# Output blocks moved into the arm of the row count, and an eviction moved into the next chunk, in a mixture-of-experts kernel

## The chip, the cores and the metric

The kernel runs on one core of one Trainium2 chip. The metric is the device time of one execution in microseconds (us), as the median of several executions. In profiles the engines are PE (TensorE, matmuls), PEld (its weight loads, which overlap the matmuls), DVE (VectorE), ACT (ScalarE), POOL (GpSimd, which also issues the indirect DMAs here) and SP (SyncE, which issues the direct DMAs). Each engine runs its own queue of instructions, and they wait for one another by semaphores.

## The reference, cut to what matters

Eight sequences of 256 tokens, 2048 tokens of width 512, all in float32, pass a gated cross-attention and then a mixture of 16 experts of which each token takes 4:

```python
x = x + tanh(g_xattn) * sigmoid_attention(layernorm(x), ctx, ctx)
xf = layernorm(x).reshape(2048, 512)
t = xf * rsqrt(mean(xf * xf) + EPS) * norm_w
vals, idx = top_k(t @ gate_w.T + gate_b, 4)
G = zeros(2048, 16).at[rows, idx].set(softmax(vals))
h = einsum('mh,eoh->emo', t, w1) + b1          # o: 2 x 512
a = minimum(h[..., ::2], 7); b = clip(h[..., 1::2], -7, 7)
act = a * sigmoid(1.702 * a) * (b + 1)
y = einsum('emi,edi->emd', act, w2) + b2
out = x + tanh(g_ffn) * einsum('me,emd->md', G, y)
```

The kernel computes each expert only for the rows that chose it, so how many rows each expert has is known only while it runs.

## The kernel before, in words

**Stages.** The first 157 us are attention, sequence by sequence, with the routing in between: each token's four experts and gates are written into a table in DRAM, sorted by expert. Two experts' first 384 rows ("early", three blocks of 128 each) follow until 226 us, while the engines also work out the plan of the rest. The rest is done in *chunks*. A chunk is up to 512 rows (four blocks of 128, `R = 4`) of one expert. The plan gives each chunk its expert, its number of blocks and its number of rows rounded up to a multiple of 16, from 256 to 512 (17 sizes, `SIZES`). There is code for 31 chunks (`MAXC`); the first 16 always run, the others inside nested `tc.If(used > c)`. With these inputs 22 run, with 448, 400, 416, 400, 384, 368, 480, 480, 288, 448, 256, 272, 288, 336, 256, 288, 256, 272, 384, 288, 256 and 320 rows.

**Plan** (L895 to L1019, on DVE, with the last early expert's matmuls beside it on PE). For each list entry it forms the row's address (`ids`, L985) and gate (`gts`, L989), turns both by PE transposes (L991, L992, into `pid`) so that a block's 128 entries lie down a column, and writes them out as `idsG` for fetching (L994), `idsT` for delivering (L998) and `gtsT` (L1000). Rows that a block does not have get an address beyond the output, and a DMA leaves such rows out. `meta` holds, for each chunk, the size's number, the number of blocks, the expert and whether it is used.

**One chunk** (`chunk(c)`), in the order of the program, which is written out by hand (`tc.manual_schedule`), so that every engine's queue has it:

- POOL gathers the next chunk's rows by four indirect DMAs (`fetch`, L1037) into `xg`.
- DVE copies the expert's bias (L1115).
- `tc.Switch` (L1118) over the 17 sizes, on PE, DVE and ACT. Each arm holds `hidden` for four column blocks `n`: 8 groups of 4 float32 matmuls (L299; in the trace a float32 matmul is two records, so a chunk has 64) with the arm's row count as their width, each group into one of the four PSUM tiles `h0` to `h3` in turn; then the evictions on DVE and ACT (L308, L316, L317, L325) into `act`. Each engine jumps into its arm and at the end out of it (the jumps bear L1213).
- SP loads w1 of the chunk after next but one (`load_hidden`, L254, 2 MB) once `hidden` has left its slot. Three slots of weights are held (`SLOTS = 3`).
- `turn`: 16 PE transposes (L284) of the next chunk's rows, evicted by four DVE multiplications (L285) into `xT`, which the next chunk's `hidden` reads.
- `expect(c + 1)` (L1061): each engine reads the next size from `meta` and gives its sequencer a hint of the arm to come.
- `output`: for each block k, `combine` (L334, 4 matmuls of 128 rows by 512 columns, 8 records, into PSUM tile `h`k), the bias added by DVE (L342, into `yb`), the gate multiplied by ACT (L347, into `yo`), and the rows added to the output in DRAM by an indirect DMA from POOL (`deliver`, L351). Block 0 always runs; blocks 1 to 3 stand each under `tc.If(blocks > k)` (L1087), and where the block is missing its Else issues four matmuls of one column on zeros (`skip`, L1066, "blanks" below). A last block with 64 rows or fewer costs a whole block.
- SP loads w2 and its bias for the chunk after next but one (`load_output`, L261 1 MB and L266 256 KB).

So PE's order in a chunk is hidden, turn, blocks 0 to 3, and the next chunk's hidden; the four PSUM tiles `h` are shared by hidden and the blocks.

Of the kernel before, what the change touches and what calls it, by code (L numbers as in the profile page):

```python
# [31 lines left out]
def kernel(  # L32
# [35 lines left out]
    SIZES = list(range(2 * P, R * P + 1, GRAIN))  # L68
    ROWS = E * NT

    out_rows = out.rearrange("b d n -> (b d) n")

# [26 lines left out]
        "yb": (moe, [P, H], 2),  # L99
        "yo": (moe, [P, H], 3),  # L100
# [33 lines left out]
    blank = const.tile([P, P], mybir.dt.bfloat16, name="blank")  # L134
    nc.vector.memset(blank, 0.0)
# [10 lines left out]
    )  # L146
    eps = const.tile([P, 1], F32, name="eps")
# [69 lines left out]
    for tag in ("xT", "act"):  # L217
        nc.gpsimd.memset(buf(tag, 0), 0.0)
# [110 lines left out]
    def combine(slot, k, lo):  # L329

        py = buf("h", k)
        act = buf("act", 0)
        for i in range(IC):
            nc.tensor.matmul(  # L334
                py,
                act[:, i, lo : lo + P],
                w2r[:, slot, i, :],
                start=(i == 0),
                stop=(i == IC - 1),
            )  # L340
        yb = buf("yb", k)
        nc.vector.tensor_tensor(yb, py, br[:, slot, :], ALU.add)  # L342
        return yb

    def scaled(k, yb, gate):
        y = buf("yo", k)
        nc.scalar.activation(y, yb, AF.Copy, scale=gate)  # L347
        return y

    def deliver(c, y, ids):  # L350
        put = nc.gpsimd.indirect_dma_start(  # L351
            out=out_rows,
            out_offset=bass.IndirectOffsetOnAxis(ap=ids, axis=0),
            in_=y,
            in_offset=None,
            compute_op=ALU.add,
            bounds_check=T - 1,
            oob_is_err=False,
        )
        for other in added.setdefault(c, []):  # L360
            tc.declare_no_dep(put.ins, other.ins, reason="a row is once in a chunk")
        added[c].append(put)
# [8 lines left out]
    with tc.tile_pool(name="att", bufs=2) as ap:  # L371
# [88 lines left out]
        def second_norm(b):  # L460
# [24 lines left out]
                else buf("yo", c)  # L485
# [267 lines left out]
        def output_early(a):  # L753
            pairs, target = early[a]
            ys = []
            for k in range(AHEAD):
                yb = combine(place_of(a - 2), k, k * P)
                ys.append(scaled(k, yb, pairs[:, k, 1:2]))
            early[a] = ys, target
# [169 lines left out]
    for h in range(2):  # L929
# [45 lines left out]
    )  # L975
    full = small("full", P, P)
# [13 lines left out]
    pid = ps_t.tile([P, 2, P], F32, tag="t", name="pid")  # L990
# [6 lines left out]
    idsT = small("idsT", P, P, dtype=I32)  # L997
    nc.vector.tensor_scalar(idsT, pid[:, 0, :], float(T), None, ALU.add)  # L998
    gtsT = small("gtsT", P, P)
    nc.vector.tensor_copy(gtsT, pid[:, 1, :])  # L1000


    meta = small("meta", P, 4, C1, dtype=I32)
# [9 lines left out]
    nc.vector.tensor_copy(meta[0:1, 1], blocks[0:1])  # L1013
    nc.vector.tensor_copy(meta[0:1, 2], expert[0:1])
    nc.vector.tensor_scalar(
        meta[0:1, 3], unit[0:1], ends[0:1, E - 1 : E], None, ALU.is_lt
# [7 lines left out]
    held_tiles["y"] = [  # L1024
# [7 lines left out]
    held_tiles["x"] = held_tiles["t"] + held_tiles["y"]  # L1032
# [30 lines left out]
    def skip(k):  # L1063

        for i in range(IC):
            nc.tensor.matmul(  # L1066
                buf("h", k)[:, 0:1],
                blank,
                blank[:, 0:1],
                start=True,  # L1070
                stop=True,
            )

    def output_block(c, k):
        q = c * R + k
        yb = combine(place_of(c), k, k * P)
        deliver(c, scaled(k, yb, gtsT[:, q : q + 1]), idsT[:, q : q + 1])

    def output(c):


        blocks = read(meta[0:1, 1, c : c + 1], R)
        for k in range(R):
            if k == 0:
                output_block(c, k)
                continue
            with tc.If(blocks > k) as more:  # L1087
                output_block(c, k)
            with more.Else():
                skip(k)  # L1090


    begun = small("begun", P, 4, SLOTS, dtype=I32)
# [4 lines left out]
    def bring(c, load, held):  # L1098

        if c not in held:  # L1100
            held[c] = (
                read(meta_of(c)[0:1, 3, c : c + 1], 1, [ET.SP]),
                read(meta_of(c)[0:1, 2, c : c + 1], E - 1, [ET.SP]),
            )
        go, e = held[c]
        load(e, c, cond=go)

    def chunk(c):

        held = {}  # L1110
# [3 lines left out]
        e = read(meta[0:1, 2, c : c + 1], E - 1, [ET.DVE])  # L1114
# [3 lines left out]
        for i in tc.Switch(size_of(c), len(SIZES), hint=f"size_{c}"):  # L1118
            for n in range(IC):
                hidden(place_of(c), bh[:, c % 2], n, 0, SIZES[i])  # L1120
        if c + SLOTS < MAXC:
            bring(c + SLOTS, load_hidden, held)
        if c + 1 < MAXC:
            for k in range(R):
                turn(k, buf("x", k), k * P)
            expect(c + 1)
        output(c)
        if c + SLOTS < MAXC:
            bring(c + SLOTS, load_output, held)

    with tc.manual_schedule():
# [12 lines left out]
        for c in range(1, SLOTS):  # L1144
            held = {}
            bring(c, load_hidden, held)
            bring(c, load_output, held)

        def rest(c):
            if c == MAXC:  # L1150
                return
            with tc.If(used > c):
                chunk(c)
                rest(c + 1)

# [61 lines left out]
```

## Time and profile before

| | |
|---|---|
| median of 3 runs | 946.06 us |
| the runs | 946.06, 950.2, 941.92 us |
| the profiled execution | 949.47 us |
| its span, first to last instruction | 947.9 us |
| mean granted PE clock | 0.987 |
| PE busy | 902.0 us, 95% |
| DVE, ACT, POOL busy | 386.1, 200.5, 287.6 us |
| moved by DMA | 144.77 MB, mean 153 GB/s |
| L299 (hidden), busy | 458.4 us, 1536 records |
| L334 (combine), busy | 261.6 us, 600 records |

How to read it: the span is the time from the first to the last instruction of one profiled execution, and the execution's own time is a little longer. A group line gives line, engine, operation, what is written and read (with buffer numbers left out), shapes and count; then busy time and mean duration in ns; then the idle time of that engine just before these instructions, and what ended most of it ("<-issue" is time in which the engine waited for nothing that the profile shows, such as a jump). Matmul records overlap, so the step from start to start (0.429 us for 512 columns) is the cost of one rather than its duration. Of the 22 chunks, 12 have a row count whose last 128-row block holds 64 rows or fewer. In all there are 69 blocks and 76 blanks.

The slices of the span show PE busy at nine tenths or more of nearly all of them:

```
PE   5999995999999999999999999999999999999992
DVE  3367565584333333333332333333333444333440
POOL 3034445434230421421312421423213232313222
```

### The profile page before, as it was taken

How to read it: one execution, taken by the hardware profiler on the slowest of the kernel's cores; microseconds unless marked ns; L12 is line 12 of the kernel's file. 1: busy time of each engine (PE TensorE's matmuls, PEld its weight loads, DVE VectorE, ACT ScalarE, POOL GpSimd, SP SyncE). 2: the span in 40 equal slices, each digit the busy share in tenths (PEclk: the TensorE clock that was granted, in tenths of full speed). 3: DMA queues.
4: the chain of work that ended last, by engine and by line, in shares of the span. 5: the costliest groups of instructions: out<-in, count | busy, mean ns of one | idle time of the engine just before them, and what ended most of it. 6: DMA issues, size and time to landing. Idle time of an engine off the chain costs nothing.

```text
span 947.9 us, 10767 instructions
## 1 busy us (share of the span) xinstructions
PE 902.0 (95%) x3134; PEld 524.3 (55%) x3134; DVE 386.1 (41%) x895; ACT 200.5 (21%) x319; POOL 287.6 (30%) x266
## 2 busy tenths in 40 slices
PE   5999995999999999999999999999999999999992
PEld 3455443555555555555444565666667677556760
DVE  3367565584333333333332333333333444333440
ACT  5567662411110110110111110111101111111110
POOL 3034445434230421421312421423213232313222
PEclk9999999999999999999999999999999999999996
DMA  5379942806864545646443654766457667634232
GB/s 170 115 160 166 164 98 69 287 7 154 294 164 159 136 122 167 168 127 192 133 118 117 180 180 128 191 208 187 164 185 216 186 177 210 207 116 123 66 71 32
DMA packets 42339, 144.77 MB, mean 153 GB/s; under 512 B 9569, under 2 KB 9697, under 8 KB 35521
## 3 DMA queue, kind: packets, MB, share of 16 engines
q1 hardware_dynamic: 20016, 98.58, 33.2%
q0 software_dynamic: 20896, 42.96, 20.7%
q8 instruction: 93, 1.52, 0.7%
q14 instruction: 198, 1.61, 0.5%
q10 hardware_dynamic: 1136, 0.10, 0.1%
HBM read 126.33 MB, written 28.38 MB: 163 GB/s over the span
## 4 chain that ended last, share of the span: by engine, by line
PE 60%; issue 14%; DMA 12%; DVE 6%; POOL 3%; ACT 2%; another core or an unknown queue 1%; POOLq 0%; DVEq 0%
PE ph L299 33%; PE ph L334 18%; DMA out_dram<-yo,idsT 11%; PE psc L434 3%; POOL out_dram L351 1%; PE pz L284 1%; PE pt L284 1%; PE pav L446 1%; DVE st L392 1%; DVE xs L453 1%; POOL xg L1037 1%; POOL table L638 1%; ACT xs L509 0%; DVE q L407 0%
## 5 line engine op out<-in xcount | busy, mean ns | idle before, releaser
L299 PE MATMUL ph<-xT,w1r 128*128 128x288 f32 (+10 forms) x1536 | 458.4, 459 | 7.9 <-DVE xT L285 4.7
L299 PEld LDWEIGHTS ph<-xT,w1r 128*128 128x128 f32 x1536 | 291.6, 191 | 166.3 <-issue 66.7
L334 PE MATMUL ph<-w2r,act 128*128 128x512 f32 x600 | 261.6, 592 | 0.6 <-issue 0.5
L351 POOL DMA_INDIRECT out_dram<-yo,idsT x69 | 108.8, 1577 | 461.4 <-ACT yo L347 446.2
L334 PEld LDWEIGHTS ph<-w2r,act 128*128 128x128 f32 x600 | 112.1, 190 | 133.1 <-issue 133.1
L316 ACT ACTIVATE ga<-ga 128x384 f32<-128x384 f32 (+10 forms) x96 | 47.3, 493 | 335.7 <-DVE ga L308 294.9
L317 DVE TENSOR_SCALAR v<-ph,bh 128x384 f32<-128x384 f32 (+10 forms) x96 | 55.6, 579 | 143.2 <-PE ph L299 134.4
L347 ACT ACTIVATE yo<-yb,gtsT 128x512 f32<-128x512 f32 x69 | 47.7, 717 | 293.4 <-DVE yb L342 284.0
L1037 POOL DMA_INDIRECT xg<-t_rows,idsG x92 | 90.7, 985 | 40.0 <-issue 23.0
L308 DVE TENSOR_SCALAR ga<-ph,bh 128x384 f32<-128x384 f32 (+10 forms) x96 | 55.6, 580 | 112.6 <-PE ph L299 83.8
L638 POOL DMA_INDIRECT table<-pair,sloti x64 | 62.5, 977 | 112.7 <-DVE mr L473 79.4
L342 DVE TENSOR_TENSOR yb<-ph,br 128x512 f32<-128x512 f32 x75 | 49.8, 686 | 67.5 <-PE ph L334 43.7
L285 DVE TENSOR_TENSOR xT<-pt,nw 128x512 f32<-128x512 f32 x46 | 29.6, 686 | 111.0 <-issue 97.5
L434 PE MATMUL psc<-kv,q 128*128 128x512 f32 x128 | 60.6, 621 | 2.4 <-ACT kvT L427 2.4
L446 PE MATMUL pav<-sc,kvT 128*128 128x512 f32 x128 | 58.7, 602 | 3.7 <-DVE mine L698 3.4
L325 DVE SCALAR_TENSOR_TENSOR act<-v,ga 128x384 f32<-128x384 f32 (+10 forms) x96 | 50.1, 522 | 14.2 <-ACT ga L316 4.6
L446 PEld LDWEIGHTS pav<-sc,kvT 128*128 128x128 f32 x128 | 23.2, 190 | 31.0 <-issue 26.5
L434 PEld LDWEIGHTS psc<-kv,q 128*128 128x128 f32 x128 | 24.4, 199 | 28.4 <-issue 24.8
L285 DVE TENSOR_TENSOR xT<-pz,nw 128x512 f32<-128x512 f32 x46 | 29.4, 681 | 0.0
L284 PEld LDWEIGHTS pt<-ident,xg 128*128 128x128 f32 x184 | 21.5, 141 | 5.8 <-issue 3.3
L284 PE MATMUL pz<-ident,xg 128*128 128x128 f32 x184 | 23.8, 273 | 0.0
L284 PE MATMUL pt<-ident,xg 128*128 128x128 f32 x184 | 23.8, 273 | 0.0
(177 smaller groups left out, 367.5 us busy)
## 6 DMA issues: line engine op xcount, KB each, us to landing
w1r<-in_L_ffn_w_dram SPq DMA_DIRECT2D x24, 2048.0 KB
w2r<-in_L_ffn_w_dram SPq DMA_DIRECT2D x27, 1024.0 KB
br<-in_L_ffn_b_dram SPq DMA_DIRECT2D x27, 256.0 KB
w1r<-in_L_ffn_w_dram SPq DMA_DIRECT2D x6, 1024.0 KB
xs<-in_x_dram SPq DMA_DIRECT2D x16, 256.0 KB
kv<-in_ctx_dram SPq DMA_DIRECT2D x16, 256.0 KB
out_dram<-xs SPq DMA_DIRECT2D x16, 256.0 KB
t_rows<-u SPq DMA_DIRECT2D x8, 256.0 KB
```

The lines of the kernel that those rows point to most:

```text
L284: nc.tensor.transpose(px[:, h, :], xg[:, ts(h, P)], ident)
L285: nc.vector.tensor_tensor(buf("xT", 0)[:, :, lo : lo + P], px, nw.unsqueeze(2).to_broadcast([P, HC, P]), ALU.mult,)
L299: nc.tensor.matmul(ph[:, 0:n], w1r[:, slot, k, h, ts(i, P)], xT[:, k, lo : lo + n], start=(k == 0), stop=(k == HC - 1),)
L308: nc.vector.tensor_scalar(ga[:, 0:n], halves[0][:, 0:n], bias[:, 0, i : i + 1], LIMIT, ALU.add, ALU.min,)
L317: nc.vector.tensor_scalar(v[:, 0:n], halves[1][:, 0:n], bias[:, 1, i : i + 1], 1.0 + LIMIT, ALU.add, ALU.min,)
L325: nc.vector.scalar_tensor_tensor(act[:, i, lo : lo + n], v[:, 0:n], 1.0 - LIMIT, ga[:, 0:n], ALU.max, ALU.mult)
L334: nc.tensor.matmul(py, act[:, i, lo : lo + P], w2r[:, slot, i, :], start=(i == 0), stop=(i == IC - 1),)
L351: put = nc.gpsimd.indirect_dma_start(out=out_rows, out_offset=bass.IndirectOffsetOnAxis(ap=ids, axis=0), in_=y, in_offset=None, compute_op ...
L434: nc.tensor.matmul(ps, qs[b][:, c, ts(n, P)], kvs[b][:, c, :], start=(c == 0), stop=(c == DC - 1),)
L446: nc.tensor.matmul(po, kvTs[b][:, n, ts(c, P)], scs[b][:, n, :], start=(n == 0), stop=(n == NCH - 1),)
L638: put = nc.gpsimd.indirect_dma_start(out=table, out_offset=bass.IndirectOffsetOnAxis(ap=sloti[:, j : j + 1], axis=0), in_=pair[:, c, k, :] ...
L1037: nc.gpsimd.indirect_dma_start(out=buf("xg", k), out_offset=None, in_=t_rows, in_offset=bass.IndirectOffsetOnAxis(ap=idsG[:, q : q + 1], a ...
```

## The change

The arm of the row count now holds more than `hidden`. As the arm is known for its size when the code is built, the number of its half blocks of 64 rows is too: `halves`, the size divided by 64, rounded up (4 to 8).

- **In the arm**, after `hidden`: the turn for the next chunk, then blocks 2 and 3 as far as the arm has them (`output_rest`), and, where `halves` is odd, a last half block of 64 rows (`combine_half`, L359): the left 256 output columns go to PSUM partitions 0 to 63 and the right 256 to partitions 64 to 127, as 8 matmuls with 64 columns of `act` as their stationary operand and 256 wide. It has its own buffer `yh`, its own list of addresses (`idsH`, of half rows of the output, `out_halves`) and of gates (`gtsH`). Each arm is filled up with blanks (L1143): 12, 4, 8, 0 and 4 of them for 4, 5, 6, 7 and 8 halves.
- **After the arm**: the weights' loads, the hint, the deliveries, and then blocks 0 and 1, which every chunk has. There is no If for a block any more, and `blocks` is not read. Blocks 0 and 1 go to `h2` and `h3`, blocks 2 and 3 to `h0` and `h1`.
- **Block 1's eviction** (bias and gate, `finish_last`, L336 and L337) is not done in its own chunk: it stands first in the next chunk's arm, on DVE and ACT, and its delivery behind that arm. After the last chunk `conclude` does both, in the Else of the If over the chunks. As the bias's slot is read until then, the load of w2 and its bias moves into the next chunk too, ahead of that of w1.
- **Deliveries**: always five in a chunk (block 1 of the chunk before, blocks 2, 3, the half block, block 0), 110 in all in place of 69; blocks that are not there have addresses beyond the output only.
- ACT scales in place (`y`, four buffers) instead of from `yb` to `yo`.
- **The plan** marks the half blocks, takes them out of `idsT`, and forms `idsH` and `gtsH`: more small DVE operations, and two more transposes into `pid` (now four), each of a product that DVE forms after `idsG` and `gtsT`. `meta` has three rows, not four.

```diff
-    def combine(slot, k, lo):
+    def finish(slot, py, y, gate):
+        nc.vector.tensor_tensor(y, py, br[:, slot, :], ALU.add)
+        nc.scalar.activation(y, y, AF.Copy, scale=gate)
+
+    def combine(slot, py, y, lo, gate, later=False):
...
+    def combine_half(slot, py, y, lo, gate):
+        act = buf("act", 0)
+        for i in range(IC):
+            for g in range(2):
+                nc.tensor.matmul(
+                    py[ts(g, HALF), 0 : H // 2],
+                    act[:, i, lo : lo + HALF],
+                    w2r[:, slot, i, ts(g, H // 2)],
+                    start=(i == 0),
+                    stop=(i == IC - 1),
+                )
+        for g in range(2):
+            nc.vector.tensor_tensor(
+                y[ts(g, HALF)],
+                py[ts(g, HALF), 0 : H // 2],
+                br[ts(g, HALF), slot, ts(g, H // 2)],
+                ALU.add,
+            )
+        nc.scalar.activation(y, y, AF.Copy, scale=gate)
...
+    for h, some in enumerate((ids, gts)):
+        nc.vector.tensor_scalar(
+            twice[:, h].rearrange("p (g s) -> p g s", g=2),
+            some[:, 0:HALF].unsqueeze(1).to_broadcast([P, 2, HALF]),
+            half,
+            None,
+            ALU.mult,
+        )
+        nc.tensor.transpose(pid[:, 2 + h, :], twice[:, h], ident)
...
+    def output_rest(c, halves):
+        for k in range(2, halves // 2):
+            output_block(c, k)
+        if halves % 2:
+            k = halves // 2
+            combine_half(
+                place_of(c), buf("h", k + 2), buf("yh", 0), k * P, gtsH[:, c : c + 1]
+            )
+        blocks = max(0, halves // 2 - 2)
+        for _ in range(3 * IC - blocks * IC - halves % 2 * 2 * IC):
+            nc.tensor.matmul(
+                buf("h", 3)[:, 0:1], blank, blank[:, 0:1], start=True, stop=True
+            )
...
         for i in tc.Switch(size_of(c), len(SIZES), hint=f"size_{c}"):
+            if c > 0:
+                finish_last(c - 1)
             for n in range(IC):
                 hidden(place_of(c), bh[:, c % 2], n, 0, SIZES[i])
+            if c + 1 < MAXC:
+                for k in range(R):
+                    turn(k, buf("x", k), k * P)
+            output_rest(c, -(-SIZES[i] // HALF))
+        if c > 0:
+            deliver_block(c - 1, 1)
+            if c - 1 + SLOTS < MAXC:
+                bring(c - 1 + SLOTS, load_output, held[c - 1])
         if c + SLOTS < MAXC:
-            bring(c + SLOTS, load_hidden, held)
+            bring(c + SLOTS, load_hidden, held[c])
         if c + 1 < MAXC:
-            for k in range(R):
-                turn(k, buf("x", k), k * P)
             expect(c + 1)
-        output(c)
-        if c + SLOTS < MAXC:
-            bring(c + SLOTS, load_output, held)
+        for k in range(2, R):
+            deliver_block(c, k)
+        deliver(c, buf("yh", 0), idsH[:, c : c + 1], out_halves)
+        output_block(c, 0)
+        deliver_block(c, 0)
+        output_block(c, 1, later=True)
```

## The prediction

> **What bounds the kernel now.** I read the page first, for the engine with the largest share and the costliest groups.
>
> ```profile
> PE 902.0 (95%) x3134; PEld 524.3 (55%) x3134; DVE 386.1 (41%) x895; ACT 200.5 (21%) x319; POOL 287.6 (30%) x266
> L299 PE MATMUL ph<-xT,w1r 128*128 128x288 f32 (+10 forms) x1536 | 458.4, 459 | 7.9 <-DVE xT L285 4.7
> L334 PE MATMUL ph<-w2r,act 128*128 128x512 f32 x600 | 261.6, 592 | 0.6 <-issue 0.5
> L351 POOL DMA_INDIRECT out_dram<-yo,idsT x69 | 108.8, 1577 | 461.4 <-ACT yo L347 446.2
> L342 DVE TENSOR_TENSOR yb<-ph,br 128x512 f32<-128x512 f32 x75 | 49.8, 686 | 67.5 <-PE ph L334 43.7
> L285 DVE TENSOR_TENSOR xT<-pt,nw 128x512 f32<-128x512 f32 x46 | 29.6, 686 | 111.0 <-issue 97.5
> ```
>
> PE leads, in two groups: hidden (L299), which the change leaves alone, and combine (L334), which it shortens. Then the windows view of the 22 chunks, 226 to 930 us, shows how much of it is PE's own (columns: stretch, length, busy of PE, PEld, DVE, ACT, POOL, clock, DMA share, GB/s).
>
> ```profile
> 226.00:930.00 704.00, 699.80 (x2430) 418.16 (x2427) 255.11 (x453) 92.29 (x159) 199.73 (x160) 1.00 0.56 161
> ```
>
> PE is idle for 4.2 of 704 us at full clock. What PE work is removed here comes off the time, and any wait that PE gains goes on it. DVE, ACT, POOL and DMA have room; only their lateness can hurt. The timeline of one chunk of 256 rows (start, length; idle before in brackets) shows the order and its gaps.
>
> ```profile
> 618.01 1.04 PE L284 MATMUL pt<-ident,xg 128*128 128x128 f32 x8
> 618.89 1.04 PE L284 MATMUL pz<-ident,xg 128*128 128x128 f32 x8
> 619.76 7.03 PE L334 MATMUL ph<-w2r,act 128*128 128x512 f32 x16
> 624.73 1.29 DVE L285 TENSOR_TENSOR xT<-pt,nw 128x512 f32<-128x512 f32 x2 [5.50 <-issue]
> 626.63 0.34 PE L1066 MATMUL ph<-blank 128*128 128x1 bf16 x8
> 627.13 1.28 DVE L342 TENSOR_TENSOR yb<-ph,br 128x512 f32<-128x512 f32 x2
> 627.87 14.93 PE L299 MATMUL ph<-xT,w1r 128*128 128x272 f32 x64 [0.90 <-DVE yb L342]
> ```
>
> DVE leaves the Switch arm at 618.83 (its sequencer's branch) and needs 5.9 us to its first L285; in 19 chunks that exit takes 5.7 to 6.3 us, in the last three, which issue no load of w1r, 2.8 to 3.5. Through it DVE is late for L342, and PE stops. The waits view adds such exits up:
>
> ```profile
> DVE xT L285 <- issue: 97.5, 18, 5.9
> ```
>
> Last, the row nearest to the new half block (two column tiles of 64): the router's L539, four column tiles of 32 columns.
>
> ```profile
> 113.73 1.88 PE L434 MATMUL psc<-kv,q 128*128 128x512 f32 x4
> 115.55 0.64 PE L539 MATMUL pl<-tT,gw 128*32 128x256 f32 x8
> 116.12 2.41 PE L446 MATMUL pav<-sc,kvT 128*128 128x512 f32 x5
> ```
>
> Eight records of 256 columns take 0.57 us from start to start. In series they would take 8 x 0.215 = 1.72 us, 0.215 being the step of a 256-column record in L299 (13.8 us / 64). So tiles in different columns run side by side, with about 0.1 us lost at a change of tiling.
>
> **The change part by part**, against the profiled execution's own 949.47 us (span 947.9); the median of the runs is 946.06, 3.4 lower.
>
> *Half blocks.* Of the 22 row counts 12 end in an odd half of 64 rows. A block is 8 records of 0.429 = 3.43 us (13.74 / 32 in a chunk of four blocks). Its half is 16 records of 256 columns in 8 pairs: 8 x 0.215 = 1.72, plus 0.2 for two changes of tiling, plus 0.2 since no row shows pairs: 2.1 us. Gain 1.33 x 12 = **-16.0**. Ends: without the second 0.2, -18.4; no overlap of the pair (16 x 0.215 + 0.2 = 3.64), +2.5. I take the value next to L539.
>
> *Waits that go.* Three stops of L299 for L342 (0.90 shown; 1.24 and 0.98 in the like chunks at 737.7 and 789.3) are, with the drain, **-3.5**: block 1's eviction no longer stands before the next chunk's first PSUM tile. Two stops of L334 at arm exits (0.66 and 0.30 between neighbouring matmuls, near 644 and 806 us) lose their places: **-0.95**. Late next: L336's eviction of block 1, below.
>
> *Blanks.* 76 now, 116 after, at 0.34 / 8 = 0.045: **+1.8**.
>
> *PE's exit in the arm of 256 rows.* PE's sequencer runs 17 records ahead when it leaves the arm (all 22 chunks). Now these are 16 L334 records of a block and more; then, for halves = 4, 12 blanks and 5 transposes, 12 x 0.045 + 5 x 0.109 = 1.1 us. The exit's branch takes 0.3, list read and hint about 1.0 to 1.1. Four such chunks lose 0.3: **+1.2**.
>
> *Code crossings.* PE's branches out of and into arms last 0.30 (mean 0.34), but one 3.3. With shorter covers I charge **+2**, between 0 (all hidden) and 5.
>
> *Plan stage.* Two more transposes stand between L992 and hidden's L299 (now 215.70 and 215.84), each behind a DVE product of 0.28, and these behind two DVE reads of pid (0.29, 0.28): PE resumes near 217.4, not 215.84. With small DVE work: **+1.8** (1 to 2).
>
> *Tail.* PE's last matmul ends at 929.5, 18.6 us before the span's end.
>
> ```profile
> 929.56 0.69 DVE L342 TENSOR_TENSOR yb<-ph,br 128x512 f32<-128x512 f32 x1 [2.80 <-PE ph L1066]
> 930.28 0.72 ACT L347 ACTIVATE yo<-yb,gtsT 128x512 f32<-128x512 f32 x1 [2.77 <-DVE yb L342]
> 931.28 1.55 POOL L351 DMA_INDIRECT out_dram<-yo,idsT  x1 [1.92 <-ACTq L1087]
> ```
>
> These three remain, but in an Else that DVE, ACT and POOL must first jump to. POOL's next jump here takes 4.4 us (933.18 to 937.62); part of it may pass while PE still computes: **+3** (0 to 5).
>
> *Block 1's eviction at the next arm's start.* New order on DVE: hidden's evictions, four L285 (0.69 each), the arm's other evictions, exit, hint, block 0, entry, then block 1's. Behind it queue all of the next chunk's evictions; PE waits for it at its fourth PSUM tile, 24 records into hidden (5.2 us at 256 rows, 6.5 at 320). With H the end of hidden, DVE's arm ends at H+3.8 for 4 halves, +4.8 for 5, +5.9 for 6, +8.1 for 7. Then come the exit, 0.9 to the hint, 5.3 to the arm's first instruction (the shortest seen), 0.7 for the eviction and 0.7 margin. PE starts the next hidden at H+9.2 for 4 halves, H+10.8 for 5. Slack before the exit is paid is 3.3 to 4.6 us in eight of the nine closest chunks, 5.2 in the ninth. An exit of 3.0, as where no load ran, costs nothing; one of 5.85 costs 17 us over nine chunks. Now the load is issued 0.6 us before the exit; then it will be 3 us or more before, so the exit meets it later. I take an exit of 4.2 to 4.3, **+4**, ends 0 and 17.
>
> *At nothing.* 110 deliveries, not 69, add 41 x 1.6 = 66 us on POOL, and these stand ahead of the next chunk's four fetches (0.985 each): POOL is busy 200 of 704 us, and a fetch has all of the next hidden (13.8 us or more) before its turn. ACT scales as many blocks as before, 12 of them half as wide. On SP the w2r load moves to the next chunk, ahead of w1r: two chunks ahead of use. DVE's and ACT's branches per block go; they ran beside matmuls.
>
> Sum: -16.0 - 3.5 - 0.95 + 1.8 + 1.2 + 2 + 1.8 + 3 + 4 = -6.65. 949.47 - 6.65 = 942.8 in such an execution; against the median, **939.4 us**.
>
> **Rivals.**
> 1. *All covers hold.* DVE's exit drops to 3.0, no crossing, no tail: -6.65 - 4 - 2 - 3 = -15.7, 930. For: those 3 chunks without a load. Against: the load still runs.
> 2. *DVE late (other side).* The exit stays 5.85 with the load in flight: 17 instead of 4 gives +6.3, 952. For: 19 of 22 exits. It decides from an exit of about 5.1 us, where the stops eat the other terms' 10.65.
> 3. *Pairs don't overlap:* +2.5 for -16, 958. For: L539 has four tiles, and no row has two. Against: L539's rate.
> 4. *PE's exit costs code.* If PE's exit takes 3.4 us as DVE's without a load, plus 1.0, it is uncovered by 3.3 for halves 4 (4 chunks), 2.6 for 5 (7), 0.5 for 6 (4), 2.0 for 7 (5): 43 us. DVE's lateness then hides in it: -6.65 - 4 - 2 - 1.2 + 43 = +29, 975. Against: all of PE's exits here take 0.3. For: none of them was so little covered, since the turn moves from behind the exit into the arm. The Trainium skill, "Runtime: NRT & Kernel Launch", section "Instruction fetch mechanics", says that a taken branch to a target outside the current two pages must fetch the page before going on. By that rule the sum would be rival 4's; DVE's exits agree with it (5.85 us), PE's 0.3 us do not.
>
> **How the numbers follow.** Forecast 0.46 (its own range 932 to 947), rival 1 0.19, rival 2 0.17, rival 3 0.05, rival 4 0.13. About 1% is what a measurement of this kernel tells from no change: below 936.6 is faster, above 955.5 slower. Faster: rival 1 and 0.18 of the forecast, 0.37. Slower: 0.09 of rival 2 (exit over 6), rival 3, 0.11 of rival 4: 0.25. Within: 0.38. The range leaves out rival 4, the worse part of rival 3 and the best of rival 1: 926 to 957.
>
> **What would show it.** Half blocks (L359): 16 records within about 2.1 us; 3.6 is rival 3. L305's fourth PSUM tile of a small chunk waiting for DVE's eviction of block 1: rival 2, by its length. L343's first record after an arm idle by 2 us or more, for no engine: rival 4. Blanks (L1143) 116 at 0.045. L299's waits for L342 gone. Last matmul to end: 18.6 plus 0 to 5. The forecast is wrong if the clock falls below 1.00 in the chunks, or if PE stops where no term stands: for xg in the turn, or for w2r.

## The result, and the profile after

The changed kernel took 935.22 us in the median of four runs (931.46 to 942.95), the kernel before 945.51 beside it: a ratio of 0.988, 95% interval 0.983 to 0.993. Run again later, on one chip with its best variants, it took 931.95 against 948.57: 0.983 (0.980 to 0.986). So the change makes the kernel 1 to 2% faster.

The profiled execution took 942.95 us with a span of 941.3; it was the longest of the four. Its page, and below it one line of the view by lines, show the change in PE's work: L343 (combine) has 504 records where L334 had 600, and L359 has 192 records of half the width. L305 is hidden, as L299 was.

```profile
PE 894.6 (95%) x3272; PEld 522.3 (55%) x3272; DVE 387.0 (41%) x915; ACT 198.4 (21%) x319; POOL 351.7 (37%) x310
L305 PE MATMUL ph<-xT,w1r 128*128 128x288 f32 (+10 forms) x1536 | 459.2, 459 | 6.3 <-DVE y L336 5.2
L343 PE MATMUL ph<-w2r,act 128*128 128x512 f32 x504 | 223.8, 596 | 1.5 <-DVE xT L291 1.5
L336 DVE TENSOR_TENSOR y<-ph,br 128x512 f32<-128x512 f32 x63 | 43.3, 691 | 213.9 <-issue 79.7
```

```profile
L359 PE MATMUL ph<-w2r,act 128*64 128x256 f32 x192 | 23.4, 385 | 0.0
```

Two idle times are new: hidden waits 5.2 us for L336, block 1's eviction, and L343 1.5 us "for xT". The windows view of the chunks has the bill.

```profile
226.00:922.00 696.00, 688.57 (x2578) 415.50 (x2577) 257.12 (x472) 89.97 (x159) 262.21 (x201) 1.00 0.58 164
```

PE is idle for 7.4 of 696 us, where it was idle for 4.2 of 704 (the columns are those of the prediction's windows line). The clearest comparison cuts each span in three: from the first transpose of the plan's lists to the first turn for the chunks, from there to PE's last matmul, and the tail behind it.

| us | before | changed | changed, second profile |
|---|---|---|---|
| start of the lists | 215.6 | 221.9 | 214.5 |
| lists to first turn | 10.6 | 13.6 | 11.9 |
| chunks, to PE's last matmul | 703.4 | 693.1 | 690.5 |
| tail | 18.3 | 12.7 | 12.4 |
| span | 947.9 | 941.3 | 929.3 |

What comes ahead of the lists is attention and routing, where the changed kernel does what the one before does but for a few small operations; in the twelve profiles of the changed kernel and its variants it ended anywhere between 208.3 and 221.9 us. This start makes 7.4 of the 12.0 us between the two profiles of the changed kernel, and puts the first of them 6.3 us behind the profile of the kernel before. A likely reason, not tested: from 14 to 214 us PE's granted clock averages 0.95 in the first profile, 0.99 in the second and 0.97 before. The three stretches that the change touches give +3.0 - 10.3 - 5.6 = -12.9 us, and +1.3 - 12.9 - 5.9 = -17.5 in the second profile; the medians give -10.3 and -16.6.

The timeline of PE in the same chunk of 256 rows that the prediction showed, and the next, has both new stops.

```profile
621.42 0.44 PE L1143 MATMUL ph<-ones 128*128 128x1 bf16 x12
622.24 7.11 PE L343 MATMUL ph<-w2r,act 128*128 128x512 f32 x16 [0.37 <-DVE xT L291]
629.90 5.74 PE L305 MATMUL ph<-xT,w1r 128*128 128x272 f32 x24 [0.56 <-DVE bh L1176]
636.46 9.43 PE L305 MATMUL ph<-xT,w1r 128*128 128x272 f32 x40 [0.82 <-DVE y L336]
...
647.57 1.95 PE L359 MATMUL ph<-w2r,act 128*64 128x256 f32 x16
649.45 0.25 PE L1143 MATMUL ph<-ones 128*128 128x1 bf16 x4
649.57 7.11 PE L343 MATMUL ph<-w2r,act 128*128 128x512 f32 x16
656.52 5.98 PE L305 MATMUL ph<-xT,w1r 128*128 128x288 f32 x24
664.20 9.97 PE L305 MATMUL ph<-xT,w1r 128*128 128x288 f32 x40 [1.70 <-DVE y L336]
```

Hidden breaks after 24 records, at its fourth PSUM tile, as foreseen. Between neighbouring matmuls these breaks are 1.0, 1.9, 1.3, 1.7 and 0.3 us, 6.2 in all, and the four stops at block 0 behind the arms of 256 rows sum to 2.1. The half block spans 1.95 us.

The 0.7 us ahead of hidden at 629.90 is put down to the bias (L1176), but hidden does not read the bias. PE's sequencer shows what it is: its branch into the arm runs from 622.98 to 629.64, beside the matmuls of blocks 0 and 1, and hidden begins 0.25 us behind it. So this is PE's own jump. Here are all of PE's branches out of and into the arms, before (L1213) and in the changed kernel (L1292), with the shortest, the median and the longest in ns.

```profile
L1213 PEldq COMPARE_BRANCH  x44: 300/342/3297, 231.2 to 912.4; - x44
L1292 PEldq COMPARE_BRANCH  x44: 300/390/6666, 240.5 to 919.5; - x44
```

The jumps out take 0.3 us in both. The jumps in take 0.3 to 3.3 us before, and 3.5 to 6.7 in the changed kernel (apart from the first and those into the arm of 256 rows); two blocks are 6.9 us, so they are hidden only just.

DVE's timeline in that chunk shows why L336 is late. Here SP issues 2 MB of w1 at 619.87, where hidden ends; DVE's last eviction in the arm ends at 623.28.

```profile
622.00 1.28 DVE L291 TENSOR_TENSOR xT<-pz,nw 128x512 f32<-128x512 f32 x2
628.86 0.69 DVE L336 TENSOR_TENSOR y<-ph,br 128x512 f32<-128x512 f32 x1 [5.58 <-DMA out_dram<-yh,idsH]
629.47 0.16 DVE L1176 COPY bh<-b1s 128x8 f32 x1
635.72 0.69 DVE L336 TENSOR_TENSOR y<-ph,br 128x512 f32<-128x512 f32 x1 [6.09 <-PE ph L305]
```

Two pauses of 6 us, neither of which is what the bracket names: DVE's sequencer records have a branch at 621.63 with the next list read at 627.94 (out of the arm), and a branch at 630.00 with its first instruction in the next arm at 635.5 (into it).

The tail, on the other hand, is shorter, with the same three instructions for the last block.

```profile
928.75 0.69 DVE L336 TENSOR_TENSOR y<-ph,br 128x512 f32<-128x512 f32 x1 [2.81 <-PEq L1229]
...
929.54 0.72 ACT L337 ACTIVATE y<-y,gtsT 128x512 f32<-128x512 f32 x1 [2.84 <-DVE y L336]
931.15 1.54 POOL L376 DMA_INDIRECT out_dram<-y,idsT  x1 [0.81 <-DMA xg<-t_rows,idsG]
```

From the start of L336 to the end of POOL's delivery they take 3.9 us, 0.7 more than before. What is gone is the 4.4 us jump that POOL made behind the delivery; its closing drain is also 1.5 us shorter (5.3 for 6.7).

### The profile page after: what moved, and what is told of

It is laid out like the page before. It is cut to its first block, busy times and chain, and to the rows that moved or that the text cites. A ratio compares the mean times of both kernels' runs of the same rounds, so it can differ in the third digit from the quotient of the medians.

```text
span 941.3 us, 10424 instructions
## 1 busy us (share of the span) xinstructions
PE 894.6 (95%) x3272; PEld 522.3 (55%) x3272; DVE 387.0 (41%) x915; ACT 198.4 (21%) x319; POOL 351.7 (37%) x310
## 5 line engine op out<-in xcount | busy, mean ns | idle before, releaser
L305 PE MATMUL ph<-xT,w1r 128*128 128x288 f32 (+10 forms) x1536 | 459.2, 459 | 6.3 <-DVE y L336 5.2
L305 PEld LDWEIGHTS ph<-xT,w1r 128*128 128x128 f32 x1536 | 292.2, 191 | 174.2 <-issue 72.0
L376 POOL DMA_INDIRECT out_dram<-y,idsT x88 | 138.7, 1576 | 388.4 <-ACT yh L373 190.0
L343 PE MATMUL ph<-w2r,act 128*128 128x512 f32 x504 | 223.8, 596 | 1.5 <-DVE xT L291 1.5
L343 PEld LDWEIGHTS ph<-w2r,act 128*128 128x128 f32 x504 | 92.9, 190 | 107.5 <-issue 103.6
L336 DVE TENSOR_TENSOR y<-ph,br 128x512 f32<-128x512 f32 x63 | 43.3, 691 | 213.9 <-issue 79.7
L337 ACT ACTIVATE y<-y,gtsT 128x512 f32<-128x512 f32 x57 | 41.1, 722 | 299.5 <-DVE y L336 291.4
L314 DVE TENSOR_SCALAR ga<-ph,bh 128x384 f32<-128x384 f32 (+10 forms) x96 | 55.5, 578 | 81.3 <-PE ph L305 74.6
L471 PE MATMUL pav<-sc,kvT 128*128 128x512 f32 x128 | 62.7, 637 | 3.8 <-DVE mine L723 3.4
L331 DVE SCALAR_TENSOR_TENSOR act<-v,ga 128x384 f32<-128x384 f32 (+10 forms) x96 | 50.1, 522 | 11.9 <-ACT ga L322 2.6
L376 POOL DMA_INDIRECT out_dram<-yh,idsH x22 | 34.0, 1545 | 7.4 <-issue 5.2
L417 DVE BATCH_NORM_STATS2 st<-xs 128x6 f32<-128x512 f32 x32 | 21.9, 685 | 10.3 <-DMA xs<-in_x_dram 9.7
```

Of the source, the lines that this page charges most:

```text
L305: nc.tensor.matmul(ph[:, 0:n], w1r[:, slot, k, h, ts(i, P)], xT[:, k, lo : lo + n], start=(k == 0), stop=(k == HC - 1),)
L314: nc.vector.tensor_scalar(ga[:, 0:n], halves[0][:, 0:n], bias[:, 0, i : i + 1], LIMIT, ALU.add, ALU.min,)
L331: nc.vector.scalar_tensor_tensor(act[:, i, lo : lo + n], v[:, 0:n], 1.0 - LIMIT, ga[:, 0:n], ALU.max, ALU.mult)
L343: nc.tensor.matmul(py, act[:, i, lo : lo + P], w2r[:, slot, i, :], start=(i == 0), stop=(i == IC - 1),)
L376: put = nc.gpsimd.indirect_dma_start(out=rows, out_offset=bass.IndirectOffsetOnAxis(ap=ids, axis=0), in_=y, in_offset=None, compute_op=ALU ...
L471: nc.tensor.matmul(po, kvTs[b][:, n, ts(c, P)], scs[b][:, n, :], start=(n == 0), stop=(n == NCH - 1),)
```

## The experiments

The theory behind them: the gain is PE work taken out by the half blocks, and part of it is given back because DVE changes arms late, since its code comes slowly while weights are being loaded. The rivals: the gain is the tail and the waits that went; DVE's jumps cost by distance; PE waits for evictions and not for its own jump. Each ran beside the kernel before; ratios are to it. The intervals of e6 to e8 are too wide to tell these by their time from the changed kernel (0.988 and 0.983); what they show is in the stretches and stops of their profiles.

**e1, block 1 evicted in its own chunk**

```diff
-            if c > 0:
-                finish_last(c - 1)
             for n in range(IC):
...
-        output_block(c, 1, later=True)
+        output_block(c, 1)
...
         def conclude(c):
-            finish_last(c)
             deliver_block(c, 1)
```

> Block 1 is evicted at the end of its own chunk and no longer at the start of the next arm; its delivery stays deferred. In the changed kernel PE stopped 6.2 us in all at L305's fourth PSUM tile (1.0, 1.9, 1.3, 1.7, 0.3) for that eviction, since DVE entered the next arm 16 to 18 us after the end of hidden: its hint came 1.3 to 1.9 us before the jump, and the jump then took 3 to 6.2 us. Theory A (the eviction is behind the late jump): without it in the arm those stops go, and the next thing that PE can meet is the eviction of the fifth group's tile h0, due 6.9 us into hidden at 256 rows; the jump comes later than before but its hint is then 3 us or more ahead, so it is short. PE's stops at L305 in the chunks under 1.5 us in all, time about 5 us below the changed kernel, near 930 (ratio to before 0.983). Rival B (DVE's jump costs its 3 to 6 us whenever it comes, hint or not): DVE enters the arm only 2 us after block 1 is evicted, plus 3 to 6, and PE stops at the fifth group for h0 instead, by 0 to 2 us in nine chunks: time as the changed kernel or up to 4 us more, 935 to 939.

940.42 us, ratio 0.991 (0.987 to 0.994). The chunks took 693.0 us, as in the changed kernel: the stops at the fourth tile are gone, and others of 0.8, 2.0, 1.4 and 1.4 us stand further into hidden, for L314, the eviction of h0, at hidden's fifth group (the view below begins at 605 us, so it has 29 of the 32 records ahead of the stop).

```profile
604.70 6.42 PE L305 MATMUL ph<-xT,w1r 128*128 128x256 f32 x29
612.96 7.17 PE L305 MATMUL ph<-xT,w1r 128*128 128x256 f32 x32 [1.84 <-DVE ga L314]
```

Rival B as far as the time goes, but not by its reason. Most of DVE's entries got *longer*, 5 to 7 us instead of 3, though the hint was 2.9 to 5.0 us ahead in the first chunks. SP's records tell why: w2's load waits for PE's last block only, so it is issued at the chunk's end. In the changed kernel's first profile, entries that begin before it take 3.0 to 4.6 us, those that begin after it 5.1 to 6.2 (in the second, two that begin 0.1 us after it take 3.4 and 3.9, the others 5.1 to 5.7); here DVE waits for block 1, so nearly all begin after it (chunk 0: load at 283.15, branch at 284.94, first instruction at 291.96). (Entries into the arm of 256 rows, 0.5 to 0.9 us but for one of 6.1 here, and the first and the last, are apart.) So the eviction's place matters little; what is on the DMA queues at that moment does. Why the hint, with which the kernel before entered most arms in 0.5 to 0.6 us, no longer saves the fetch stays open.

**e2, delivered there too, with no Else**

```diff
         output_block(c, 1)
+        deliver_block(c, 1)
...
-            with tc.If(used > c) as more:
+            with tc.If(used > c):
                 chunk(c)
                 rest(c + 1)
-            with more.Else():
-                conclude(c - 1)
```

> As the kernel with block 1's eviction in its own chunk, and its delivery there too, so that the If over the chunks has no Else and nothing is left to conclude. The change's tail, from the end of PE's last matmul to the end of the span, was 12.7 us, against 18.4 before. Theory A (before, each engine's jump past the code of the chunks that are not run came behind the last delivery, 4.4 us on POOL; with the Else it is made while PE still computes the last two blocks): here the jump is behind the last delivery again and the tail is 17.5 to 19 us, so 5 to 6 us more than the kernel of the same run with the deferred delivery. Rival B (the tail's length is that of the last DMAs' landing, or chance from run to run): the tail is 12 to 14 us as in the changed kernel. Elsewhere the two kernels do the same.

939.37 us, 0.991 (0.987 to 0.995); tail 15.6 us, against 12.9 in e1. POOL jumps from 919.99 to 923.13 around its last delivery, where e1 has none. Between the two theories: 2.7 of the 5.6 us come back with the jump. The other 2.7 I did not settle; in the kernel before, the last delivery stands in an If of its own, and there POOL's jump took 4.4 us, 3.1 here, and its closing drain 6.7 us, 5.4 here.

**e3, no half blocks**

```diff
-        for k in range(2, halves // 2):
+        blocks = -(-halves // 2) - 2
+        for k in range(2, 2 + blocks):
             output_block(c, k)
-        if halves % 2:
-            k = halves // 2
-            combine_half(
...
```

> The last odd half block is done as a whole block again, in the arm, with the ordinary lists; all else as in the changed kernel (48 blanks more). Theory A (the gain is PE work taken out, 12 times 1.45 us as the changed kernel's trace has it): time 15 to 18 us above the changed kernel, about 951, so above the kernel before by some 5 us: moving alone costs. PE's stops for block 1's eviction shrink by 1 to 2 us in the chunks of 5 halves, whose arms become 1.45 us longer on PE. Rival B (the gain is mostly the shorter tail and the waits that went, 5.7 and 4.5 us, and the half blocks are given back by DVE's lateness): time at most 8 us above the changed kernel, so below 944.

950.43 us, 1.002 (0.9995 to 1.004): no faster than before. Theory A, and the account closes: the chunks take 707.8 us, 4.4 more than before (stops of 5.8 us in place of 4.5, and twice the blanks), the lists 3.0 more, the tail 5.3 less, +2.1 in all; the medians differ by 2.1 (948.32 before). Moving the blocks brings nothing; it makes the half blocks possible, and these are worth 14.7 us of the chunks.

**e4, the half block's two sides one after the other**

```diff
-        for i in range(IC):
-            for g in range(2):
+        for g in range(2):
+            for i in range(IC):
                 nc.tensor.matmul(
                     py[ts(g, HALF), 0 : H // 2],
```

> In the half block the four matmuls of the left columns come first and then the four of the right, so that neighbouring matmuls use the same column tile but for one place; the work is the same. Theory A (two column tiles run side by side only where neighbouring records are in different tiles): 16 records take about 3.5 us in place of 1.9, and the 12 half blocks cost 18 to 20 us more: time about 952 to 955. Rival B (a 64-column matmul of 256 columns costs half of its 0.215 us in any order, or PE looks further ahead): 16 records take 1.9 to 2.0 us as they do now, time as the changed kernel, 935.

945.27 us, 0.996 (0.992 to 0.9995). Neither theory: 16 records span 2.86 us, between 1.95 and 3.5.

```profile
647.64 2.86 PE L359 MATMUL ph<-w2r,act 128*64 128x256 f32 x16
```

The raw records show how. In the changed kernel they start in pairs, 6 ns apart, every 0.216 us. Here the left side's first four start alone, then four pairs run (a right record starting within 0.06 us of a left one), then the right's last four are alone: 12 steps in place of 8. So two column tiles do run side by side without their records being neighbours, but the right side's first record starts only with the left's fifth: order decides 0.9 us of each half block.

**e5, no loads of w1 in the chunks**

```diff
-        if c + SLOTS < MAXC:
-            bring(c + SLOTS, load_hidden, held[c])
```

> Leaves out the loads of w1 within the chunks (the chunks after the third compute with the weights of the first three), nothing else. It measures DVE's jump out of the arm (from its branch to the next list read) without 2 MB in flight. In the changed kernel that took 6.1 to 6.3 us for 4 halves, 5.1 to 6.4 for 5, 3.2 to 4.1 for 6, 2.8 to 3.6 for 7, 2.75 for 8, and 2.8 and 3.0 in the last chunks of 5 and 4 halves, which load nothing. Theory A (the load issued at the end of hidden, landing 8 to 9 us later, holds up the fetch of DVE's code; the small arms end first and so fall into it): all exits take 2.7 to 3.2 us whatever the arm, PE's stops for block 1's eviction fall from 6.2 to under 1 us, time 5 to 6 us below the changed kernel. Rival B (the small arms stand furthest from the Switch's end, and the jump costs by distance): exits of 4 and 5 halves stay at 5 to 6 us, and the stops with them; time as the changed kernel.

925.77 us, 0.980 (0.969 to 0.990). The chunks after the third compute with the weights of the first three. DVE's 22 exits took 2.75 to 3.3 us, in every arm: theory A, and distance falls. The eviction of block 1 now only waits for PE; here is the same chunk.

```profile
612.89 1.28 DVE L291 TENSOR_TENSOR xT<-pz,nw 128x512 f32<-128x512 f32 x2
616.89 0.69 DVE L336 TENSOR_TENSOR y<-ph,br 128x512 f32<-128x512 f32 x1 [2.72 <-PE ph L343]
617.50 0.16 DVE L1176 COPY bh<-b1s 128x8 f32 x1
621.27 0.69 DVE L336 TENSOR_TENSOR y<-ph,br 128x512 f32<-128x512 f32 x1 [3.61 <-PE ph L343]
```

All of PE's stops in hidden are gone and the four at block 0 are left (0.51 to 0.58). The chunks fall by 8.0 us to 685.2, a little more than the stops of the first profile of the changed kernel in and ahead of hidden (6.9), and by 5.3 from its second.

**e6, blanks ahead of the turn**

```diff
+            fill(-(-SIZES[i] // HALF))
             if c + 1 < MAXC:
                 for k in range(R):
                     turn(k, buf("x", k), k * P)
...
-                buf("h", 3)[:, 0:1], blank, blank[:, 0:1], start=True, stop=True
+                buf("h", 1)[:, 0:1], blank, blank[:, 0:1], start=True, stop=True
```

> The blanks of each arm stand before the turn, not at the arm's end (into tile h1, which is free by then). Same work. In the changed kernel PE stopped four times at block 0 after the arms of 4 halves, 0.5 to 0.6 us each, 2.1 in all; the trace names DVE's xT as the releaser. Theory A (the stop is PE's own jump, list read and hint, about 1.3 us, after a sequencer that is 17 records ahead; 12 blanks at 0.025 and 5 transposes cover 0.85 us only): with 17 transposes and hidden's last record behind it the cover is 1.75 us or more, and the four stops go: 2 us less. Rival B (PE waits for DVE's evictions of the turn, as the releaser says): the stops stay, and are longer by what the blanks took, 0.2 us. Beyond that no change in either.

931.25 us, 0.985 (0.976 to 0.994). The four stops at block 0 are gone, so they were PE's own jump and list read, whatever releaser the trace infers. But the chunks took 695.5 us, 2.4 to 5.0 more than the changed kernel's: PE came to the fourth tile earlier, DVE did not, and the stops there grew (2.2, 2.1, 0.5, 1.0, 2.3, 0.2). That makes good the 2.1 us gained at block 0; the rest of the loss is PE's own jump into the next arm, not covered for 1.5 us in all (0.7 in the changed kernel's first profile), and 1.7 us of slow records behind the stop of 2.3.

**e7, w1 loaded behind the next arm's start**

```diff
                 bring(c - 1 + SLOTS, load_output, held[c - 1])
-        if c + SLOTS < MAXC:
-            bring(c + SLOTS, load_hidden, held[c])
+                bring(c - 1 + SLOTS, load_hidden, held[c - 1])
```

> The load of w1 is issued one chunk later, right behind that of w2 and the bias, which waits for block 1's eviction in the next arm; so 3.25 MB are in flight from some 6 us into hidden, and none is issued at hidden's end. Theory A (loads in flight hold up DVE's code): DVE's exits of the longer arms fall to 2.7 to 3 us, those of 4 and 5 halves (16 to 18 us after the start of hidden, the load being about 14 us long from its issue near 6) to 3 to 5; its entries, which now meet no load, stay at 3 us. PE's stops for block 1's eviction fall from 6.2 to 1 to 3 us: time 3 to 5 us below the changed kernel. Rival B (distance or order of the code): exits as now, stops as now, time within 1 us of the changed kernel. A third way: 3.25 MB at once hold up the gather of the next rows as well, PE waits for xg in the turn, and it is slower by some us.

932.27 us, 0.988 (0.979 to 0.997). All of DVE's exits took 2.8 to 3.3 us and its entries 2.9 to 3.8 (0.5 into the arm of 256 rows; the first, beside the first loads, 6.9), with the same code and the same bytes as the changed kernel, only at another time. PE's jumps into the arms took 3.8 us at most, instead of 6.7. That DVE waits for code can be read from the trace's DMA packets, which no view lists: in 21 of these 22 exits two 8 KB packets of the instruction queue (q14 on the page) begin, the first 1.0 to 1.3 us behind the branch and the second 1.6 to 1.9. In the eight slow exits of the changed kernel's first profile the first begins only after 2.8 to 3.8 us. The packets themselves take 0.3 to 0.6 us in both, so it is their start that the load delays.

No stop for block 1 is left; the chunks take 689.0 us, 4.1 and 1.5 less than in the changed kernel's two profiles, which differ by 2.7 between themselves. The third way holds too, in small: PE waits for gathered rows in the turns of four small chunks.

**e8, the two transposes one column block later**

```diff
-        nc.tensor.transpose(pid[:, 2 + h, :], twice[:, h], ident)
...
     hidden_early(1, 2)
+    for h in range(2):
+        nc.tensor.transpose(pid[:, 2 + h, :], twice[:, h], ident)
...
     hidden_early(1, 3)
```

> The two new transposes of the plan stage, and the lists that come of them, stand behind one more column block of hidden (whose matmuls are 5.2 us of PE work), so that PE does not wait for DVE's products. From the first transpose of the lists to the first turn of chunk 0 took 10.6 us before and 13.6 in the changed kernel and in four variants of it, though the stop for the products is 0.97 us and the two transposes 0.22: 1.6 us more lie in the five records of hidden after the stop, each at twice its step of 0.32. Theory A (PE's second stop in 3 us makes its clock drop for those records, so the stop costs 3.0 in all and not 1.2): here the way takes 10.7 to 11 us and the time is 2.7 us below the changed kernel. Rival B (the slow records come of the first stop, 1.83 us, which before had as well): 1.2 us less only, to 12.4.

931.71 us, 0.983 (0.974 to 0.993). Lists to first turn: 10.82 us, theory A. The slow records are gone with the stop; in e6 and in the second profile of the changed kernel, though, the same stop had none behind it (11.9 us). So they follow the stop often, not always; they are the granted clock, as the last section shows.

**e11, the changed kernel again; e9, the three edits together; e10, and the gather issued earlier** (one chip)

```diff
         if c + 1 < MAXC:
             expect(c + 1)
+        if c + 2 < MAXC:
+            for k in range(R):
+                fetch(c + 2, k)
```

> The changed kernel as it is, beside the two that follow, on one chip, and for a second profile of it. Theory (the profiled execution of the changed kernel was long by its attention and routing, not by what was changed: the first transpose of the lists began at 221.9 us, against 208 to 219 in eight variants with the same code up to there): the stretch from chunk 0's first turn to PE's last matmul is again 692 to 695 us and the tail 12.5 to 13.1, while the start of the lists differs by several us. Ratio to before 0.983 to 0.990. Rival: the stretch of the chunks or the tail differs by more than 2 us, so that one profile of each does not carry the account.

> Blanks before the turn, loads of w1 behind the next arm's start, and the two transposes behind one more column block: the three edits that were tried alone. Alone, by their profiles, the chunks took 4.1 us less with the moved loads and 2.4 us more with the blanks first (the four stops at block 0 went, but PE was ahead of DVE and stopped longer for block 1's eviction), and the lists 2.8 us less. Theory (with DVE's exits at 2.8 us nothing waits for DVE any more, and the four stops of 0.5 to 0.8 us, 2.8 in all with the loads moved, go for good): chunks 686 to 687.5 us, lists 10.8, time 9 to 10 us below the changed kernel of the same call. Rival (PE, earlier by 2.8 us, meets DVE or the gathered rows earlier, and stops as long there): chunks 688 to 690, time 6 to 7 us below the changed kernel.

> As the kernel with all three edits, and the gather of the rows of the chunk after next is issued behind the arm, as soon as the turn has left its buffers, instead of at the start of the next chunk behind five deliveries. With the loads moved, PE stopped for the gathered rows in five small chunks, 2.1 us in all with the drains. Theory (the gather was late because it ran beside 3.25 MB of loads): those stops go, chunks 684 to 686 us, 2 us below the kernel with all three edits. Rival (the gather now runs where DVE fetches its code for the exit, and holds that up as the load of w1 did): DVE's exits of the small arms return to 4 us or more and PE's stops for block 1's eviction with them: time as all three or up to 4 us more.

931.95 us for the changed kernel (0.983), 931.00 for e9 (0.981, 0.978 to 0.983), 926.62 for e10 (0.976, 0.974 to 0.979). In e11 the chunks were 690.5 us, 2.7 less than in the first profile, over the 2 us that I had set: its stops were 6.7 us instead of 9.1, so one profile carries the account to 3 us, no better. e9's rival held in kind, and cost more than it said: chunks 691.0 instead of 688 to 690, and a time only 1 us below the changed kernel's, because the gathered rows were late in five chunks and a late turn leaves PE's jump uncovered again (three stops of 1.0 us). e10 is the theory in full: its chunks take 683.4 us, and the only stop left is 0.3 us. Its rival shows too, but PE does not meet it: with the gather beside them DVE's exits took 3.0 to 4.5 us. The tail is 14.7 us, 1.9 more than e7's; 0.9 of these because DVE's last jump ends 1.1 us behind PE's last matmul (0.2 in e7).

```profile
228.00:911.00 683.00, 682.77 (x2562) 412.39 (x2560) 255.94 (x464) 90.39 (x159) 262.22 (x204) 1.00 0.59 168
```

In e10's chunk of 256 rows nothing stands between hidden, turn, blocks 0 and 1 and the next hidden (of which the view has the first 28 records).

```profile
611.73 0.44 PE L1145 MATMUL ph<-ones 128*128 128x1 bf16 x12
612.03 1.07 PE L290 MATMUL pt<-ident,xg 128*128 128x128 f32 x8
612.94 1.04 PE L290 MATMUL pz<-ident,xg 128*128 128x128 f32 x8
613.81 7.03 PE L343 MATMUL ph<-w2r,act 128*128 128x512 f32 x16
620.68 6.58 PE L305 MATMUL ph<-xT,w1r 128*128 128x272 f32 x28
```

It is 5.3 us faster than the changed kernel on that chip and 22 us faster than before, 2.4%.

## Why the prediction was right, and where its terms were off

The time lay 4 us from the forecast of 939.4, inside its own range. The mechanism was right: PE's matmuls are the bound, the half blocks take work out (e3), and DVE's late change of arms gives some back (e5, e7). The sum was less good than the time: it forecast 6.65 us off the kernel before, and the medians gave 10.3, and 16.6 in the later run. The latter is the figure of rival 1 (15.7) but not its mechanism, since DVE's exits did not drop to 3.0. That the time came so near is in part luck: against the first profile the tail was 8.6 us better than forecast, while the plan stage, PE's exit and block 1's eviction were 4.3 us worse. The terms, in us, against that profile:

| term | predicted | measured |
|---|---|---|
| half blocks | -16.0 | -17.4 |
| waits that go | -4.45 | -4.5 |
| blanks | +1.8 | +1.0 |
| PE's exit in the arm of 256 rows | +1.2 | +2.1 |
| code crossings on PE | +2 | +0.7 (second profile +1.7) |
| plan stage | +1.8 | +3.0 (second profile +1.3) |
| tail | +3 | -5.6 |
| block 1's eviction | +4 | +6.2 (second profile +2.7) |
| sum | -6.65 | -14.5 |

The three stretches gave -12.9; the 1.6 us between that and the sum are mostly steps of about 0.1 us in the first record where PE changes from blanks or half blocks to whole ones (22 such places), which I had not charged.

- **Half blocks.** A block and a half block take 5.41 us where two blocks took 6.86: 1.45 saved each, 12 times. The second 0.2 us, added since no row showed pairs, was not needed: pairs run at the full rate of L539's four tiles.
- **Waits that go.** None of the five came back. e1 shows that L305's fifth tile would have been the next to wait.
- **Blanks.** A further blank costs 0.025 us; 0.34 / 8 has the end of the group in it.
- **PE's exit.** Right in kind and place (four stops, e6); 0.5 us each, not 0.3. Rival 4 is refuted by the same rows: behind the other arms, down to a cover of about 1.8 us, PE does not stop, so its jump out costs what its branch rows said and no 3.4.
- **Code crossings.** Right in kind, and inside its range. The reading under it was wrong: 0.34 is the median of the 44 branches, not their mean, and the row hides that the jumps in took 0.3 to 3.3 us already. In the changed kernel they take up to 6.7 us (7.1 in the second profile), and PE stops where the two blocks ahead do not cover that: 0.7 us once, and 1.2 and 0.5 in the second profile.
- **Plan stage.** The stop and the transposes were 1.2 us; what was missing is five records of hidden behind it, at a granted clock of 0.50.
- **Tail.** The step that failed, with the wrong sign (the tail before, put at 18.6 us, was 18.3). I put the jump into the Else behind PE's last matmul and took it as an addition to a way out that stays. In fact DVE, ACT and POOL decide "no further chunk" while PE computes the last two blocks, and the code behind the Else is the end; the long jump that stood behind the last delivery is hidden (2.7 us by e2, the rest open).
- **Block 1's eviction.** Rival 2's mechanism at a third of its price. The exits of 4 halves were even worse than its 5.85 us (6.1 to 6.3), and those of 5 halves 5.1 to 6.4, but only these arms end inside the load. With 6 to 8 halves they took 2.75 to 4.1, not 5.85, and entries into the arm of 256 rows took 0.5 to 0.9, not the 5.3 us with the hint that I had put in. So nine stops became five (four in the second profile).

"At nothing" held: 110 deliveries and the later load of w2 stopped PE nowhere. That w2's load would meet DVE's entry I had not seen.

The Trainium skill, "Runtime: NRT & Kernel Launch", section "Instruction fetch mechanics", says that a taken branch out of the two current pages waits for a fetch of the target. DVE agrees: 2.75 to 3.3 us for each exit, with no load of w1 near (e5). That the fetch takes twice as long beside a load is in these runs.

## What to carry to other kernels

Where one engine is the bound, take work off it and then list its gaps by what ended them; each new gap tells which other engine has become late, once the releaser that the view names has been held against the engines' own branches (the stops put down to DVE's xT and bias were PE's own jumps). Moving a load by some microseconds can be worth more than moving the code. Compare stretches that the change touches rather than spans, and take a second profile before a few microseconds are explained. When a way out of nested branches is moved, ask who is still busy while it is taken.

## What the runs showed of the hardware that was not expected

- **Code fetch and bulk loads meet.** DVE's jump out of an arm took 2.75 to 3.3 us with no load issued near it and 5.1 to 6.4 with 2 MB issued up to 4 us before; its jump into an arm 2.9 to 3.8 in e7 (up to 4.6 elsewhere), and 5 to 7 with w2's 1 MB just issued. PE's jump into an arm took 3.8 us at most in e7, and up to 6.7 beside the loads. The hint ahead of it did not help there (e1: 3 to 5 us ahead in the first chunks, 6.4 to 7.2 us all the same).
- **DVE enters the first arm of the Switch in 0.5 us** in most cases, where the others take 2.7 or more: of the 48 entries into it (256 rows) in the twelve profiles of the changed kernel and its variants, 47 took 0.5 to 1.4 us and one 6.1 (e1). That its place is the reason was not tested.
- **Two column tiles overlap beyond neighbours**: 16 records in 1.95 us alternating, 2.86 us in two runs of eight, 3.5 if in series.
- **A stop can be followed by half the clock.** Behind two stops of 1.83 and 0.97 us at the lists, three to five records ran at half speed in seven of the nine profiles that have this pair (up to 1.7 us). They are PE's granted clock: in these seven it stands at 0.5 for 3.4 us right there, and not in the two others. Here it is in the first profile.

```profile
223.70:227.10 3.40, 3.40 (x7) 1.68 (x6) 3.09 (x12) 0.00 (x0) 2.48 (x4) 0.50 0.52 153
```

In the chunks the clock fell in the same way behind a stop of 2.3 (e6) and one of 2.6 us (e2), with six to eight slow records, but not behind one of 2.6 (e4) or those of 2.2 and less.
